# Two graph layers on one core: the order of VectorE's work within a turn, and of the last steps

## Chip, cores, metric

The kernel runs on one core of a Trainium2 chip. The metric is device time in microseconds (us), the median of three runs of the whole program. A core has five engines that run their own instruction streams and wait for one another by semaphores: TensorE (PE in the profile; its weight loads are PEld), VectorE (DVE), ScalarE (ACT), GpSimd (POOL) and SyncE (SP, which here only issues transfers).

## The reference

64 graphs of 256 nodes with 256 features go through two layers. Everything is 32-bit floating point.

```
layer 0, per graph:  h = x
  twice:  Wh = h @ W;  e = leaky_relu(Wh @ a[:F] + (Wh @ a[F:]).T)
          h = softmax(where(adj > 0, e, -9e15), axis=1) @ Wh
  h = layernorm(x + h);  h = layernorm(h + relu(h @ w_ff1 + b_ff1) @ w_ff2 + b_ff2)
layer 1, per graph:  8 heads of 32 features
  attn = softmax(q k^T / sqrt(32));  out = sum_r (attn * (adj == r)) @ (src @ Wv[r])
  x = layernorm(src + out @ Wo);     layernorm(x + gelu(x @ W1 + b1) @ W2 + b2)
```

The adjacency holds zeros and ones only, so of the four relations of layer 1 two occur. The kernel uses that, and tests on the chip whether it holds; with other data a general path would run.

## The kernel before

**Tiling.** Two graphs make a pair: 512 nodes, which is T = 4 blocks of 128 partitions (NB = 2 blocks per graph, G = 2 graphs). There are NG = 32 pairs.

**Pipeline over turns.** `turn(y_, x_, z)` runs three pairs at once: layer 1 of pair `y_`, the feed-forward part of layer 0 of pair `x_ = y_ + 1`, and the two attention steps of layer 0 of pair `z = y_ + 2`. In the code capital `Y`, `X`, `Z` are the dictionaries of these pairs; near the end `X` or `Z` is None. `middle` is true in turns 1 to 30, in which `X` exists and `y_` isn't 0. Ahead of turn 0 stands a prologue that loads weights and brings pairs 0 and 1 to the point where turn 0 expects them; it spreads the folding of norm weights into the next weights over its waits (`next(fold)`). An output norm that a turn leaves open is put on `waiting` and finished in the next turn.

**Products with seven multiplications.** Large products are computed block-wise with seven products in place of eight. `hidden_seven` makes the hidden layer of a feed-forward part: it subtracts quarters of the features first (`sub`, line 881, tile `tt`), and then goes through named steps. A digit names a product and a letter the half of the hidden features: "2a" is product 2 for half a. Two banks of PSUM per half, `one` and `two` (tiles `h1a` and `h1b`), take the products; after each product the bank is copied by ACT (line 911) or added by DVE (line 908, `taken`), and the next product of the same bank is accumulated on top of what is there, so it can't start before that copy or addition has read the bank. Products 1, 6, 7, 4 share bank `one`, products 2, 5, 3 bank `two`. "ra", "sa", "ca", "da" are activations on ACT. `Projections` does the same for q, k ("q1" and so on) and v ("v1" and so on), with DVE additions at line 1039 and ACT copies at line 1042. `HiddenOut` makes the second half of a feed-forward part; its `sums` are DVE operations at line 974, its `add` is line 996.

**Attention of layer 1.** There are four quads (graph b, half m of the heads), numbered 0 to 3. `scores(n)` is the score product (`sp`, line 1075) and the exponential on ACT (`e`, line 1084); `masks(n, (a,))` multiplies two heads by the adjacency on DVE (`ea`, line 1088, one instruction of 128x1024); `totals(n)` adds the two node blocks (`es`, line 1093); `sums(n)` are the products with v (`po`, line 1103, first with `e`, then with `ea`) and, last, with ones (`zo`, line 1106, from `es`); `shares(b)` divides.

**Norms.** `moments` runs bn_stats and bn_aggr on DVE (lines 826, 827), per block of 128 rows; `norm` calls it for the blocks not yet done and then computes the reciprocal root on GpSimd (lines 837, 838, and 840 for the last norm); `offsets` is one small DVE instruction (`nm`, line 845) that needs the root; `applied_norm` applies mean and root per block on ACT (line 855) or, on request, on GpSimd (line 852). `affine` multiplies by the norm's weight and adds its bias on DVE (lines 864, 867, 128x1024 each).

**Transposed features.** `normed_features` transposes 32x32 blocks on DVE (line 694), and twelve SyncE transfers and four GpSimd copies put the blocks in place (tile `hT`). `to_features` does it with TensorE transposes (line 674) and two copies out of PSUM (line 675), one by ACT and one by DVE unless told otherwise. `with_ones` then sets one row of 512 to one, a memset on GpSimd (line 686): that row carries the bias.

**What sets the order.** `tc.manual_schedule` fixes the order of the code on the engines that it lists. In turns 0 to 30 these are PE, SP, DVE and ACT; in turn 31 and in the prologue PE and SP. Engines that aren't listed are ordered by a planner with its own costs; GpSimd always is.

In a middle turn the code gives the following order in the part that edits 1 to 3 of the change touch (shortened; a bar separates steps, dots stand for left-out ones):

```
            scores(0, (0, 1)) ... v5 q6, v6, masks(0, (0,))
            q3 q7 | masks(0, (2,)) | v7 | totals(0) | v3 q4 v4
            first_hidden (four subtractions) | norm(w, 3, wy) | scores(1)
            masks(1, (0,)) | offsets | masks(1, (2,)) | totals(1) | sums(0) | 2a 1a .. 5a ..
            scores(2) | sums(1) | 6a | shares(0) | 3a | masks(2, (0,)) | 2b ra 1b 7a
            masks(2, (2,)) | 5b sa 6b 4a | totals(2) | 3b rb 7b
```

Of the kernel before, what the change touches and what calls it, by code (L numbers as in the profile page):

```python
# [385 lines left out]
def narrow_path(  # L386
# [281 lines left out]
    def to_features(src, name, copies=(nc.scalar.copy, nc.vector.tensor_copy)):  # L668

        dst = work.tile([P, KB, TN], F32, tag="hT", name=name)  # L670
        for k in range(KB):
            ps = bank(f"{name}p{k}")
            for t in range(T):
                nc.tensor.transpose(ps[:, t * P:(t + 1) * P], src[:, t, k * P:(k + 1) * P], ident)
            copies[k](dst[:, k, :], ps)  # L675
        return [dst[:, k] for k in range(KB)]
# [7 lines left out]
    def with_ones(hT):  # L684

        nc.gpsimd.memset(hT[KB - 1][one], 1.0)
        return hT
# [142 lines left out]
    def norm(u, l, y, blocks=range(T), mv=None, rest=range(NB, T)):  # L830

        n, t0 = f"{u}_{l}_{blocks[0]}", blocks[0]
        bt = slice(t0, t0 + len(blocks))
        mv = moments(u, l, y, blocks if mv is None else rest, mv)
        rs = work.tile([P, T], F32, tag="rs", name=f"rs{n}")
        nm = work.tile([P, T], F32, tag="nm", name=f"nm{n}")
        nc.gpsimd.tensor_scalar(rs[:, bt], mv[:, bt, 1], EPS, 0.0, op0=ALU.add, op1=ALU.add)  # L837
        nc.gpsimd.tensor_tensor(rs[:, bt], rs[:, bt], mhalf[:, bt], ALU.pow)  # L838
        if l == 3:
            nc.gpsimd.tensor_add(high[:, bt], high[:, bt], mv[:, bt, 0])  # L840
        return blocks, mv, rs, nm
# [5 lines left out]
    def applied_norm(y, blocks, mv, rs, nm, part=None, gpsimd=False):  # L847
        if part is None:
            offsets(blocks, mv, rs, nm)
        for t in part or blocks:  # L850
            if gpsimd:
                nc.gpsimd.tensor_scalar(y[:, t, :], y[:, t, :], rs[:, t:t + 1], nm[:, t:t + 1],
                                        op0=ALU.mult, op1=ALU.add)
                continue
            mark["normed"] = nc.scalar.activation(y[:, t, :], y[:, t, :], AF.Identity,  # L855
                                                  bias=nm[:, t:t + 1], scale=rs[:, t:t + 1])

    def affine(y, g_, b_):

        times(y, g_)  # L860
        plus(y, b_)
# [145 lines left out]
    class Projections:  # L1007
# [17 lines left out]
        def out(s, x, o, b):  # L1025
            if x == "q":
                return s.qk[:, o, :, b * N:(b + 1) * N]
            return s.v[:, b * NB:(b + 1) * NB, o * F:(o + 1) * F]
# [173 lines left out]
    def first_hidden(x_):  # L1202

        X = g[x_]
        hT = X["hT"]
        if x_ == 0:
            hT = [h.rearrange("p (t a r) -> p t a r", t=T, r=32) for h in hT]
        X["h1"] = work.tile([P, FB, TN], F32, tag="h1", name=f"h1{x_}_0", bufs=1)
        tt = work.tile([P, Q, KB, T, 32], F32, tag="yt", name=f"tt{x_}_0", bufs=1)
        return hidden_seven(x_, 0, hT, wf1s, bf1, AF.Relu, X,  # L1210
                            tt.rearrange("p q k t r -> p (q k t r)"))
# [5 lines left out]
    def turn(y_, x_, z):  # L1217
# [9 lines left out]
        def scores(n, heads=range(HPB)):  # L1227
            pe[n], e[n] = weighted(y_, *quads[n], q, k_, Y["aT"])
            powers(n, heads)
# [4 lines left out]
        def masks(n, *pairs):  # L1234
            masked(*e[n], *pairs)
# [10 lines left out]
        def shares(b):  # L1246
            divided(y_, b, *acc[b], oT)
# [5 lines left out]
        def first(names, ends=0):  # L1253

            if X:
                steps(names)
            else:
                for _ in range(ends):
                    piece()
# [3 lines left out]
                                            ("PE", "SP", "DVE", "Activation")[:4 if X else 2]})  # L1263
        with order:
            p.sums()
            if X:
                n = X.pop("n")
                offsets(*n)
# [35 lines left out]
            if X:  # L1304
                masks(0, (0,))
            if middle:
                p("q3 q7")
                masks(0, (2,))
                p("v7")
            else:  # L1310
                p("q6 v6 q7 v7")
                if X:
                    masks(0, (2,))
# [4 lines left out]
                    masks(0)  # L1318
                    totals(0)
            p("v3 q4 v4" if middle else "q4 v4")  # L1320
            steps = first_hidden(x_) if X else None
            if waiting:
                last = norm(w, 3, wy, mv=last)
            scores(1)
            masks(1, (0,))
            if waiting:
# [19 lines left out]
            if not X:  # L1346
                with behind("out"):
                    shares(0)
            masks(2, (0,))
            first("2b ra 1b 7a")  # L1350
            masks(2, (2,))
            first("5b sa 6b 4a")
            totals(2)
# [44 lines left out]
            if Z:  # L1398
                out(1)
                Z["m"].scores(0)  # L1400
                Z["m"].scores(1)
                Z["m"].exp(0)
                Z["m"].exp(1)
                out.sums(4)
                offsets(*n)
                out(2)
                applied_norm(y, *n, range(T))
                Z["m"].masks(0)
                out(5)
                Z["m"].masks(1)  # L1410
                Z["m"].shares()
            elif X:
                out(5)
                out.sums(3)
            if not Z:
                applied_norm(y, *n)
            else:
                Z["m"].scaled(WH)
                nc.scalar.activation(work.tile([P, 1], F32, tag="ve", name=f"ve{y_}"), mhalf[:, 0:1], AF.Gelu)
# [36 lines left out]
            if Z:  # L1456
                second("2a 1a")
                n = norm(x_, 1, X["y"], mv=n, rest=range(NB + 1, T))
                second("2b 1b ca 6a")
                offsets(*n)  # L1460
                applied_norm(X["y"], *n, [0])
                applied_norm(X["y"], *n, [2, 3], True)
                second("5a")
                applied_norm(X["y"], *n, [1])
                affine(y, rg3, rb3)
                second("6b 5b cb")
                X["hT"] = normed_features(x_, 1, X["y"], natural=True)
                second("7a 7b sa sb 3a da 3b db 4a 4b")
            else:
                if X:  # L1470
                    n = norm(x_, 1, X["y"], mv=n, rest=range(NB + 1, T))
                second("2a 1a 2b 1b")
                second("5a 5b")
                if X:
                    applied_norm(X["y"], *n)
                second("3a 3b 6a 6b ca cb da db 7a 7b")
                if X:
                    affine(y, rg3, rb3)
                    X["hT"] = with_ones(to_features(X["y"], f"h2T{x_}", (nc.vector.tensor_copy,) * 2))
                second("sa sb 4a 4b")  # L1480
            if y_ >= NG - 2:
                pieces = out_pieces(y_, y, h1)
                if X:
                    left.append(pieces)
                    affine(X["y"], rg2, rb2)
                else:
                    for _ in pieces:
                        pass
                return
# [25 lines left out]
            out(4)  # L1515
            waiting.append((y_, y))

    waiting = []

    with tc.manual_schedule(engines={mybir.EngineType.PE, mybir.EngineType.SP}):  # L1520
        for stage in (early_first, project, first_softmax):
            stage(0)
        early_first(1)
        next(fold)
        for stage in (project, first_softmax):
            stage(1)
        first_sums(0)
        next(fold)
        second_softmax(0)
        first_sums(1)  # L1530
        next(fold)
        second_softmax(1)
        for b in range(G):
            second_sums(0, (b,))
            normed(0, 0, g[0]["y"], range(b * NB, (b + 1) * NB))
        next(fold)
        g[0]["hT"] = to_features(g[0]["y"], "h1T0")
        for u in range(2):
            checked(u, g[u]["aq"])
        affine(g[0]["y"], rg1, rb1)  # L1540
        load_x(2)
        load_rows(2)
        load_adjacency(2)
        first_hidden(0)("2a 1a 2b 1b 5a 5b 3a 3b 6a ra 6b rb 7a sa 7b sb 4a 4b")
        first = HiddenOut(0, 0, g[0]["y"], g[0]["h1"], wf2s, out_sums(0, 0))
        first.sums(1, 2, 4, 3)
        first(1, 2, 5, 6, 3)
        normed(0, 1, g[0]["y"], range(NB))
        first(7, 4)
        normed(0, 1, g[0]["y"], range(NB, T))  # L1550
        g[1]["n"] = norm(1, 0, g[1]["y"], mv=second_sums(1))
        g[0]["hT"] = with_ones(to_features(g[0]["y"], "h2T0"))
        affine(g[0]["y"], rg2, rb2)
        next(fold)
        for u in range(NG):
            turn(u, u + 1, u + 2)
# [54 lines left out]
```

## Time and profile before

| | |
|---|---|
| median of 3 runs | 3021.93 us (3021.1 to 3023.58) |
| the profiled execution's own time | 3021.42 us |
| its span in the profile | 3019.7 us |
| granted TensorE clock | 0.995 |
| PE busy | 2965.3 us (98%), 22192 instructions |
| DVE busy | 2609.3 us (86%), 5025 instructions |
| ACT busy | 1729.2 us (57%) |
| POOL busy | 642.9 us (21%) |
| prologue, start of turn 0 (first product at line 1055) | 103.5 us |
| turn 0 | 98.2 us |
| turns 1 to 29 | 90.9 to 92.9 us each, mean 91.6 |
| turn 30; turn 31 to the end | 75.9 us; 86.8 us |

A turn is taken in the timeline from its first matmul at line 1055 to that of the next turn. In a timeline each line holds the start in us, the time from the first start to the last end of equal instructions in a row, the engine, the line of the kernel, the operation, the tiles written and read with their shapes, the count, and in brackets how long the engine was idle just before and who ended that. Matmuls overlap: an entry of four matmuls of 128x256 is 1.03 us long when they start 0.216 us apart and the last takes 0.379 us, and the next entry then begins 0.86 us after it. A matmul that starts later than that has waited, even where the entries still overlap and no idle time is printed.

### The profile page before, as it was taken

Reading aid. Unit: us, or ns where it says so; the run is one execution under the profiler, and the core shown is the slowest. Engines: PE = TensorE matmul, PEld = TensorE weight load, DVE = VectorE, ACT = ScalarE, POOL = GpSimd, SP = SyncE. Lnnn points to the kernel's source line nnn. Section 1 sums busy time; section 2 is a strip of 40 time slices with the busy share of each in tenths; the row PEclk is TensorE's granted clock in tenths of the full one; section 3 lists DMA queues with packets and bytes.
Section 4 is the critical chain, followed back from the end, with each engine's and each line's share of the span. In section 5 each row is a group of like instructions: output and inputs, shape, how many; then the busy total and the mean of one; then the engine's idle time right before and its main releaser. Section 6 shows DMA issues by size and latency. Waiting matters only on the chain.

```text
span 3019.7 us, 58579 instructions
## 1 busy us (share of the span) xinstructions
PE 2965.3 (98%) x22192; PEld 2492.9 (83%) x22192; DVE 2609.3 (86%) x5025; ACT 1729.2 (57%) x3564; POOL 642.9 (21%) x928
## 2 busy tenths in 40 slices
PE   7999999999999999999999999999999999999998
PEld 6788888888888888888888888888888888888876
DVE  5788888889888889898889888898988898888887
ACT  4455655655655656565555556556556555555553
POOL 4222211222211222211222112222112222112211
PEclk8999999999999999999999999999999999999999
DMA  5011111211111211112111112111112111121000
GB/s 149 13 31 41 38 39 25 45 38 40 36 30 36 45 37 40 33 27 43 38 41 37 39 26 45 38 40 37 34 33 45 38 40 33 27 43 38 22 10 16
DMA packets 428404, 113.26 MB, mean 38 GB/s; under 512 B 364586, under 2 KB 427604, under 8 KB 428116
## 3 DMA queue, kind: packets, MB, share of 16 engines
q1 hardware_dynamic: 418076, 102.20, 15.5%
q10 hardware_dynamic: 8984, 6.19, 0.8%
q8 instruction: 178, 2.92, 0.4%
q0 software_dynamic: 1056, 1.05, 0.1%
q14 instruction: 110, 0.90, 0.1%
HBM read 56.78 MB, written 16.78 MB: 24 GB/s over the span
## 4 chain that ended last, share of the span: by engine, by line
PE 76%; DVE 13%; SPq 4%; issue 2%; DMA 2%; POOL 2%; ACT 1%; ACTq 0%; DVEq 0%; POOLq 0%
PE yf L988 25%; PE h1a L899 12%; PE h1b L899 8%; PE po L1103 5%; SPq L713 4%; PE v L1055 4%; PE qk L1055 4%; PE xpp L740 4%; PE yop L811 4%; PE hpp L800 3%; PE ygp L811 3%; PE sp L1075 2%; DVE ea L1088 2%; DVE h L908 2%; PE zo L1106 1%
## 5 line engine op out<-in xcount | busy, mean ns | idle before, releaser
L855 ACT ACTIVATE y<-y,nm,rs 128x256 f32<-128x256 f32 x452 | 243.5, 592 | 142.3 <-DVE nm L845 137.9
L1088 DVE TENSOR_TENSOR ea<-e,aT 128x1024 f32<-128x1024 f32 x256 | 307.3, 1212 | 2.8 <-ACT e L1084 2.8
L1084 ACT ACTIVATE e<-sp 128x512 f32<-128x512 f32 x512 | 270.5, 596 | 27.4 <-PE sp L1075 20.8
L911 ACT COPY h<-h1b 128x512 f32<-128x512 f32 x262 | 152.3, 582 | 199.1 <-PE h1b L899 196.7
L837 POOL TENSOR_SCALAR rs<-mv 128x4 f32<-128x4 f32 (+1 forms) x134 | 56.6, 422 | 968.3 <-DVE mv L827 787.6
L917 ACT ACTIVATE h<-h,cols 128x256 f32<-128x256 f32 x512 | 221.7, 501 | 38.9 <-DVE h L908 38.1
L1042 ACT COPY qk<-qk 128x512 f32<-128x512 f32 x128 | 74.4, 581 | 291.9 <-PE qk L1055 291.9
L711 POOL COPY hT<-yt 32x256 f32<-32x256 f32 x244 | 211.4, 867 | 140.2 <-DVE yt L694 129.0
L826 DVE BATCH_NORM_STATS2 st<-y 128x6 f32<-128x256 f32 x512 | 208.1, 408 | 5.6
L908 DVE TENSOR_TENSOR h<-h1a,h 128x512 f32<-128x512 f32 x262 | 173.1, 679 | 40.8 <-PE h1a L899 33.0
L996 DVE TENSOR_TENSOR y<-yf,y 128x256 f32<-128x256 f32 x448 | 184.7, 412 | 17.1 <-PE yf L988 16.6
L1116 POOL TENSOR_TENSOR low<-low,rq 128x16 f32<-128x16 f32 x64 | 14.0, 218 | 740.1 <-DVE rq L1115 740.1
L867 DVE TENSOR_TENSOR y<-y,rb 128x1024 f32<-128x1024 f32 (+1 forms) x130 | 167.0, 1284 | 3.2
L742 ACT COPY xp<-xpp 128x260 f32<-128x260 f32 x128 | 45.5, 386 | 195.1 <-PE xpp L740 195.0
L864 DVE TENSOR_TENSOR y<-y,rg 128x1024 f32<-128x1024 f32 (+1 forms) x130 | 155.8, 1198 | 1.2 <-ACT y L855 1.1
L1093 DVE TENSOR_TENSOR es<-e 128x1024 f32<-128x1024 f32 x128 | 155.7, 1216 | 0.0
L838 POOL TENSOR_TENSOR rs<-rs,mhalf 128x4 f32<-128x4 f32 (+1 forms) x134 | 146.8, 1095 | 8.3
L1075 PE MATMUL sp<-qk 32*128 32x256 f32 x2048 | 146.6, 400 | 0.0
L1103 PE MATMUL po<-ea,v 128*32 128x256 f32 x2048 | 137.8, 379 | 0.8 <-DVE ea L1088 0.7
L1103 PE MATMUL po<-e,v 128*32 128x256 f32 x2048 | 136.3, 384 | 0.0
L899 PE MATMUL h1a<-tt,wf 128*128 128x256 f32 x512 | 131.3, 380 | 0.0
L740 PE MATMUL xpp<-gwe,xT 128*128 128x260 f32 x512 | 128.4, 395 | 2.0 <-ACT xT L675 2.0
(284 smaller groups left out, 7648.9 us busy)
## 6 DMA issues: line engine op xcount, KB each, us to landing
hT<-yt SPq DMA_DIRECT2D x912, 32.0 KB, 1.9
y<-in_x_dram SPq DMA_DIRECT2D x32, 512.0 KB, 4.7
xq<-in_x_dram SPq DMA_DIRECT2D x240, 64.0 KB, 2.2
aq<-in_adj_dram SPq DMA_DIRECT2D x240, 64.0 KB, 2.4
out_dram<-y SPq DMA_DIRECT2D x30, 512.0 KB
hT<-yt ACTq DMA_DIRECT2D x180, 32.0 KB, 1.9
wf<-in_L_gnn_w_ff_dram SPq DMA_DIRECT2D x2, 1024.0 KB, 7.4
w<-in_L_gnn_W_dram SPq DMA_DIRECT2D x2, 1024.0 KB, 7.7
```

The source lines that it names most:

```text
L711: nc.gpsimd.tensor_copy(to, at)
L740: nc.tensor.matmul(ps[:, :WX], hT[k][:, t * P:(t + 1) * P], gwe[:, k, :], start=(k == 0), stop=(k == KB - 1))
L811: nc.tensor.matmul(ps[:, i * F:(i + 1) * F], lhs(t, k), rhs(b, k), start=(k == 0), stop=(k == n - 1))
L855: mark["normed"] = nc.scalar.activation(y[:, t, :], y[:, t, :], AF.Identity, bias=nm[:, t:t + 1], scale=rs[:, t:t + 1])
L899: nc.tensor.matmul(ps[:, i * N:(i + 1) * N], w_[:, f * P:(f + 1) * P], m, start=first and i == 0, stop=True, skip_group_check=True)
L908: mark["added"] = nc.vector.tensor_tensor(out(h, o, b), pair(ps), out(h, o, b), ALU.add)
L917: nc.scalar.activation(y, y if ps is None else ps[:, i * N:(i + 1) * N], func, bias=bi[:, f:f + 1])
L988: nc.tensor.matmul(s.ps[n][:, i * F2:(i + 1) * F2], a[:, k, i * P:(i + 1) * P], w_[:, k, :], start=n in (1, 2, 5) and i == 0 and k == 0, s ...
L1055: nc.tensor.matmul(ps[:, i * N:(i + 1) * N], l, r, start=n in (1, 2, 5) and i == 0, stop=True, skip_group_check=True)
L1084: nc.scalar.activation(e[:, a, :], ps[a], AF.Exp, scale=isd)
L1088: nc.vector.tensor_tensor(ea[:, a:a + 2, :], e[:, a:a + 2, :], ab[:, None, :].to_broadcast([P, 2, NB * N]), ALU.mult)
L1103: nc.tensor.matmul(po[hp, m * N:(m + 1) * N], vs[:, hp], w[:, a, j * N:(j + 1) * N], start=(n == 0), stop=(n == len(terms) - 1))
```

## The change

Seven edits.

1. In the middle turns the second half of quad 0's masks goes behind the addition of v7 on DVE.
2. In the middle turns the last norm's remaining statistics (`norm(w, 3, ...)`: two bn_stats and two bn_aggr on DVE, three small operations on GpSimd) go ahead of the four feature subtractions of `first_hidden`.
3. In turns 0 to 30 the first half of quad 2's masks goes behind the addition of 1b and ahead of that of 7a.
4. In turn 30 `sums(3)` of the feed-forward output goes between product 5 and its addition.
5. In turn 30 the norm of pair 31 isn't applied by four ACT operations in a row: block 0 and block 1 stay on ACT, ahead of the copies of 3a and 3b, and blocks 2 and 3 go to GpSimd.
6. The affine steps of the prologue (pair 0) and of turn 30 (two of them) are kept on a list, `late`, and are written behind the feature subtractions of the next turn's `Projections`. In turn 31, where DVE isn't ordered by hand, the planner places them: in the built program one of turn 30's two affine steps then stands in the middle of turn 30, around the first bn_stats of pair 31, and the other among turn 31's feature subtractions.
7. In the prologue both copies of `to_features` are on ACT; in the built program the memset of the ones row then stands on GpSimd between the two scalings of `w1` (line 603) and no longer behind both.

```diff
             p.sums()
+            while late:
+                affine(*late.pop(0))
             if X:
                 n = X.pop("n")
                 offsets(*n)
...
             if middle:
-                p("q3 q7")
+                p("q3 q7 v7")
                 masks(0, (2,))
-                p("v7")
...
             p("v3 q4 v4" if middle else "q4 v4")
-            steps = first_hidden(x_) if X else None
             if waiting:
                 last = norm(w, 3, wy, mv=last)
+            steps = first_hidden(x_) if X else None
             scores(1)
...
+            first("2b ra 1b")
             masks(2, (0,))
-            first("2b ra 1b 7a")
+            first("7a")
             masks(2, (2,))
...
             elif X:
-                out(5)
+                out.product(5)
                 out.sums(3)
+                out.add(5)
...
                 second("5a 5b")
                 if X:
-                    applied_norm(X["y"], *n)
-                second("3a 3b 6a 6b ca cb da db 7a 7b")
+                    offsets(*n)
+                    applied_norm(X["y"], *n, [0])
+                second("3a")
                 if X:
-                    affine(y, rg3, rb3)
+                    applied_norm(X["y"], *n, [1])
+                second("3b")
+                if X:
+                    applied_norm(X["y"], *n, [2, 3], True)
+                second("6a 6b ca cb da db 7a 7b")
+                if X:
                     X["hT"] = with_ones(to_features(X["y"], f"h2T{x_}", (nc.vector.tensor_copy,) * 2))
...
                 if X:
                     left.append(pieces)
-                    affine(X["y"], rg2, rb2)
+                    late.append((y, rg3, rb3))
+                    late.append((X["y"], rg2, rb2))
...
-    waiting = []
+    waiting, late = [], []
...
-        g[0]["hT"] = with_ones(to_features(g[0]["y"], "h2T0"))
-        affine(g[0]["y"], rg2, rb2)
+        g[0]["hT"] = with_ones(to_features(g[0]["y"], "h2T0", (nc.scalar.copy,) * 2))
+        late.append((g[0]["y"], rg2, rb2))
```

The order of TensorE's matmuls and of SyncE's transfers is the same in both programs.

## Prediction

> **What bounds the kernel now.** The page comes first, for who is busy:
>
> ```profile
> PE 2965.3 (98%) x22192; PEld 2492.9 (83%) x22192; DVE 2609.3 (86%) x5025; ACT 1729.2 (57%) x3564; POOL 642.9 (21%) x928
> ```
>
> PE is the bound, and idle for 54 us, but busy entries overlap. So I read matmul starts in the timeline: four products of 128x256 take 0.86 us, and a later next entry has waited. Laying turns 1 to 29 over each other, the shortest (turn 9) has 90.92 us and the mean is 91.57. Three places in turn 16 show where PE waits for DVE. First, v4, in PE's timeline and then DVE's:
>
> ```profile
> 1587.32 1.03 PE L1055 MATMUL qk<-tq,wqk 128*128 128x256 f32 x4
> 1588.27 1.13 PE L1055 MATMUL v<-wv,tq 128*128 128x256 f32 x4
> ```
> ```profile
> 1585.00 1.48 DVE L1039 TENSOR_TENSOR qk<-qk,qk 128x512 f32<-128x512 f32 x2 [1.40 <-PE qk L1055]
> 1586.40 1.22 DVE L1088 TENSOR_TENSOR ea<-e,aT 128x1024 f32<-128x1024 f32 x1
> 1587.53 0.68 DVE L1039 TENSOR_TENSOR v<-v,v 128x512 f32<-128x512 f32 x1
> ```
>
> v4 is due at 1587.32 + 0.86 = 1588.18. It starts at 1588.27, 0.06 after the addition of v7 has left its bank at 1588.21. Its entry lasts 1.13 in place of 1.03: after a wait the second matmul starts 0.32 after the first, not 0.216. So this costs 0.09 + 0.10 = 0.19, in all of turns 1 to 30. The addition stood behind a mask.
>
> Second, the stretch around the transposed features, on DVE and then PE:
>
> ```profile
> 1591.17 0.43 DVE L881 TENSOR_TENSOR tt<-hT 128x256 f32<-128x256 f32 x1 [1.22 <-issue]
> ...
> 1592.64 0.42 DVE L826 BATCH_NORM_STATS2 st<-y 128x6 f32<-128x256 f32 x1
> ...
> 1593.72 1.19 DVE L1088 TENSOR_TENSOR ea<-e,aT 128x1024 f32<-128x1024 f32 x1
> 1596.19 0.16 DVE L845 SCALAR_TENSOR_TENSOR nm<-mv,rs 128x4 f32<-128x4 f32 x1 [1.27 <-POOL rs L838]
> 1596.27 1.22 DVE L1088 TENSOR_TENSOR ea<-e,aT 128x1024 f32<-128x1024 f32 x1
> 1597.41 1.22 DVE L1093 TENSOR_TENSOR es<-e 128x1024 f32<-128x1024 f32 x1
> ```
> ```profile
> 1597.53 1.07 PE L1103 MATMUL po<-ea,v 128*32 128x256 f32 x16
> 1598.68 0.64 PE L1106 MATMUL zo<-es,ones 128*32 128x256 f32 x8
> ```
>
> DVE waits for the transfers of `hT` (in the list of waits, tt waits 55 us for DMA over the kernel), then works through everything behind it, waiting 1.27 more for GpSimd's root. `zo`, due at 1598.39, waits for `es`. The transfers land between 14.76 us (turn 9) and 16.11 us (turn 4) after the turn's start, 16.82 in turn 30; turn 4 is 1.36 us longer than turn 9. From here to 6b DVE leads and PE follows.
>
> Third, 6b, on PE and then DVE:
>
> ```profile
> 1603.70 1.03 PE L899 MATMUL h1b<-tt,wf1s 128*128 128x256 f32 x4
> 1605.12 1.13 PE L899 MATMUL h1a<-tt,wf1s 128*128 128x256 f32 x4 [0.39 <-DVE h L908]
> ```
> ```profile
> 1603.25 1.21 DVE L1088 TENSOR_TENSOR ea<-e,aT 128x1024 f32<-128x1024 f32 x1
> 1604.38 1.28 DVE L908 TENSOR_TENSOR h<-h1a,h 128x512 f32<-128x512 f32 x2
> ```
>
> 6b is due at 1604.56 and starts 0.56 late, as the addition of 1b stood behind a mask. Even turn 9 loses 0.16 here, and 0.10 at the second matmul.
>
> **The Trainium skill.** "Perfetto Trace Analysis", section Identifying the Most-Contended Engine, says that matmul busy share doesn't measure the distance to the limit; the trace agrees (98% busy, yet the waits above). "TensorE: Matmul & The Clock Gate", section Step-by-step, has matmuls in program order with only weight loads pulled ahead: one late addition holds everything behind. In the trace nothing overtakes v4 or 6b. "SBUF — State Buffer", section Who interferes with whom, has DVE and GpSimd sharing a port pair as an exclusive lock. The trace fits: GpSimd's first root operation (line 837) took 1.00 us beside a mask at 1594.00, but 0.24 at 1576.95; in the prologue DVE's `nm` took 1.23 beside a GpSimd addition, not 0.16.
>
> **Edit 1, v7 ahead of the mask.** v7's product begins at 1585.59. An addition follows its product's begin by 1.07 (7b in turn 0: 140.36 and 141.43), so at 1586.66, done at 1587.34: v4 doesn't wait. Gain 0.19 x 30 turns = 5.8 us. DVE now idles some 0.2 for v7; mask, `es` and v3's addition come 0.26 later, the latter at 1589.52. The mask is needed by `po` at 1591.29 only.
>
> **Edit 2, statistics first.** They take 1593.72 - 1592.64 = 1.08 us. Behind v3's addition they run from 1590.2 to 1591.3, in the wait for `hT`. The subtractions start when both are there, 1591.3 (before 1591.17); 5a needs the first of them at 1594.53. The mask of quad 1 starts 1.47 after them, 1592.7 in place of 1593.72. GpSimd's three operations are moved past nothing of its own, since its queue is empty; they took 2.4 from the last statistic to `nm`, so the root is there at 1593.8, when the mask ends. Then `es` runs 1595.1 to 1596.3, 2.3 earlier, and `zo` (due 1598.2) waits no more. If the port keeps GpSimd out until the mask is done, `nm` waits its 1.27 again and `es` ends at 1597.6, still in time. Even with transfers as late as 16.1, `zo` is met. What goes is the excess over turn 9 between `hT` and 6b: on average 0.19 at `zo` and 0.26 at 6b, 0.44 x 29 = 12.9, plus 1.6 in turn 30: 14.5 us.
>
> **Edit 3, 1b ahead of the mask.** With DVE no longer late, 1b's addition begins 1.07 after its product and ends at +1.75; 6b is due at +2.59 and doesn't wait. Gain beside that of edit 2: 0.26 x 30 = 7.8 us. Behind the waiting addition stands the mask, and behind that 7a's addition, which 4a waits for: 1.07 + 0.60 + 1.13 + 0.68 = +3.48, and 0.06 to the start, +3.54. 4a is due at 4 x 0.864 = +3.46. **This is a new wait**: 0.08 + 0.10 = 0.18 in turns 0 to 30, a loss of 5.7 us. It could be nothing (-0) or, if 1b's addition is late by some tenths, twice that.
>
> **Edits 4 to 7.** Edit 4 costs nothing: `nm` at 2909.50 waits for GpSimd's root, and the next addition is behind it. Edit 7 and the prologue's part of 6: at 108.98 PE has waited 1.80 for the ones row, which stood behind 4.47 us of weight scaling. It now stands behind half of that, near 106.6. Then q5 waits for q2's addition, behind two affine instructions on DVE (2.4 us) and `nm`. Nothing to 1.8; I take 0.5, as `nm` comes hardly earlier. The second copy costs ACT 0.59, inside its idle 3.38. Edits 5 and 6 in turn 30: 7a waited 1.89 at 2927.15 for copies behind four ACT norms (2.07), and q1 waited 1.26 at 2933.01 for copies behind an affine. Both shrink, but the affine now in turn 30's middle puts 2.3 us of DVE ahead of the subtractions: 5a, due at 2919.84, waits some 1.5, and GpSimd's two blocks (1.48 each in earlier turns) end near 2928.8, ahead of the transposes. Between 2 lost and 1 gained; I take 0.
>
> **Sum.** 5.8 + 14.5 + 7.8 - 5.7 + 0.5 = 22.9, of the profiled execution's own 3021.42 (span 3019.7): 2998.5. The median is 0.5 above that execution: 2999 us.
>
> **Rivals.** (a) *The gain is partly given back at 4a* (chance 0.15). Where 1b's addition starts late, because the division ahead of it does, the mask between makes 4a wait as long as 6b did. For it: every instruction from 1591 to 1606 on DVE hangs together. Against: the 2 us of reserve at `es`. Then 7.8 and about a third of 14.5 are lost: 3012. (b) *No change, the transfers are next* (0.08). In 5 of 29 turns the first product of the second hidden layer waits 0.3 to 1.4 us for `hT`, on average 0.12. If PE arrives 0.75 earlier and the features don't, it waits there: 3021. Against: `tt` and the norm behind it move with PE, as both follow 7b. (c) *Slower, by the same transfers* (0.06). They share SyncE's queue with the next pair's loads; if the new times make them meet in every turn, each waits like turn 8 (1.36). It decides from a mean wait of 0.12 + 0.75 + 0.2 = 1.1 us per turn; at 1.36 the cost is 1.24 x 29 = 36, less 22.9: 3035. Nothing in the trace makes it likely. (d) The change doesn't do what it says: the affine step was to move behind turn 31's subtractions and lands in turn 30. That is in the sum; with GpSimd holding the port it costs 4, 3003. It belongs to the main case.
>
> **Numbers.** A measurement tells about 0.2%, 6 us, from no change. Main case 0.71: 2993 (no wait at 4a) to 3006 (twice that wait, and turn 30's 2 us). With (a) the range is 2992 to 3014. Faster 0.86, same 0.08, slower 0.06.
>
> **What would show it.** In the profile after: v4 0.86 behind q4; no wait of `zo`; 6b 0.86 behind 5b; 4a some 0.95 behind 6b, with an entry of 1.13; all middle turns within 0.1 of 90.65 except for the waits on `hT`. Turns still spread by the transfers' times would refute edit 2's account, a 4a later than 1.2 behind 6b that of edit 3.

## The result, and the profile after

| | before | after |
|---|---|---|
| median of 4 runs | 3022.76 us (3021.1 to 3026.34) | 3003.71 us (3001.51 to 3007.76) |
| ratio of after to before | | 0.9937, 95% interval 0.992 to 0.9954 |
| the profiled execution: own time; span | 3021.42; 3019.7 us | 3007.76; 3006.1 us |
| start of turn 0 | 103.5 us | 103.7 us |
| turn 0 | 98.16 us | 100.45 us |
| turns 1 to 29: shortest; mean; sum | 90.92; 91.57; 2655.5 us | 90.73; 91.07; 2641.1 us |
| turn 30; turn 31 to the end | 75.86; 86.7 us | 74.08; 86.8 us |

The change gains 19 us by the medians; 22.9 were predicted. The profiled execution after is the slowest of its four runs, 4.05 us above their median, which has to be kept in mind when its sums are read. It gains only 13.6 us of span, 14.4 of them in turns 1 to 29 and 1.8 in turn 30, while turn 0 loses 2.3 and the prologue 0.2.

In the page of the kernel after, first busy time and then the chain of waits that ended last:

```profile
PE 2952.3 (98%) x22192; PEld 2493.3 (83%) x22192; DVE 2614.8 (87%) x5024; ACT 1728.7 (58%) x3563; POOL 622.7 (21%) x930
...
PE 90%; DVE 5%; DMA 2%; ACT 1%; issue 1%; POOL 1%; SPq 0%; ACTq 0%; POOLq 0%; DVEq 0%
```

PE's share of the busy time is again 98%, so the busy line shows nothing of the gain. The chain does: before, it gave PE 76% and DVE 13%, since it was so often followed back through a late addition or mask.

Turn 16 again, in the timeline of PE:

```profile
1582.15 1.03 PE L1055 MATMUL qk<-tq,wqk 128*128 128x256 f32 x4
1583.01 1.03 PE L1055 MATMUL v<-wv,tq 128*128 128x256 f32 x4
...
1592.17 1.05 PE L1103 MATMUL po<-ea,v 128*32 128x256 f32 x16
1593.04 0.61 PE L1106 MATMUL zo<-es,ones 128*32 128x256 f32 x8
...
1598.00 1.03 PE L899 MATMUL h1b<-tt,wf1s 128*128 128x256 f32 x4
1598.86 1.03 PE L899 MATMUL h1a<-tt,wf1s 128*128 128x256 f32 x4
1599.89 1.13 PE L899 MATMUL h1a<-tt,wf 128*128 128x256 f32 x4
```

v4 stands 0.86 behind q4, `zo` 0.87 behind `po`, 6b 0.86 behind 5b: the three waits of before are gone. 4a, the last line, comes 1.03 behind 6b instead of 0.86, and its entry is 1.13 long: the new wait, 0.17 + 0.10 = 0.27 us. And in the timeline of DVE:

```profile
1581.56 0.69 DVE L1039 TENSOR_TENSOR v<-v,v 128x512 f32<-128x512 f32 x1 [0.24 <-PE v L1055]
1582.16 1.22 DVE L1088 TENSOR_TENSOR ea<-e,aT 128x1024 f32<-128x1024 f32 x1
...
1586.41 0.44 DVE L881 TENSOR_TENSOR tt<-hT 128x256 f32<-128x256 f32 x1 [0.22 <-issue]
...
1589.06 0.15 DVE L845 SCALAR_TENSOR_TENSOR nm<-mv,rs 128x4 f32<-128x4 f32 x1
...
1590.27 1.21 DVE L1093 TENSOR_TENSOR es<-e 128x1024 f32<-128x1024 f32 x1
...
1593.72 0.72 DVE L1114 STREAM_TRANSPOSE rz<-zo 128x512 f32<-128x512 f32 x1 [0.48 <-PE zo L1106]
...
1597.41 0.69 DVE L908 TENSOR_TENSOR h<-h1a,h 128x512 f32<-128x512 f32 x1 [0.62 <-PE h1a L899]
1598.02 1.22 DVE L1088 TENSOR_TENSOR ea<-e,aT 128x1024 f32<-128x1024 f32 x1
1599.15 0.68 DVE L908 TENSOR_TENSOR h<-h1a,h 128x512 f32<-128x512 f32 x1
```

`nm` waits for no root any more, and `es` is done 1.5 us ahead of `zo`. DVE now waits for PE at `rz` (a transpose of what `zo` made) and at 1b's addition, where before PE waited for DVE. The last three lines are the new wait: 1b's addition, the mask and 7a's addition run without a gap, the last ends at 1599.83, and 4a starts 0.06 later.

Of turns 1 to 29, 21 now take 90.73 or 90.74 us; the scatter with the arrival of the first `hT` of a turn is gone. What is left in the other eight is mostly waits of one later product, the first of layer 1's second feed-forward part, for the transfers of its `hT`. In PE's timeline of turn 1:

```profile
268.92 1.10 PE L899 MATMUL h1b<-hT,w 128*128 128x256 f32 x4 [2.38 <-DMA hT<-yt]
```

and 0.23 us per turn on average, after 0.11 before. (Turns 21 and 25 lose 0.3 to 0.4 us later, at line 988; such losses stood in eight turns before, too.) Turn 0 is taken up with the experiments, since its loss was not foreseen.

### The profile page after: what moved, and what is told of

The parts are those of the page before. It is cut to its first block, busy times and chain, and to the rows that moved or that the text cites. A ratio compares the mean times of both kernels' runs of the same rounds, so it can differ in the third digit from the quotient of the medians.

```text
span 3006.1 us, 58577 instructions
## 1 busy us (share of the span) xinstructions
PE 2952.3 (98%) x22192; PEld 2493.3 (83%) x22192; DVE 2614.8 (87%) x5024; ACT 1728.7 (58%) x3563; POOL 622.7 (21%) x930
## 4 chain that ended last, share of the span: by engine, by line
PE 90%; DVE 5%; DMA 2%; ACT 1%; issue 1%; POOL 1%; SPq 0%; ACTq 0%; POOLq 0%; DVEq 0%
PE yf L988 24%; PE h1a L899 15%; PE h1b L899 11%; PE po L1103 7%; PE v L1055 7%; PE qk L1055 6%; PE sp L1075 4%; PE ygp L811 3%; PE xpp L740 3%; PE yop L811 3%; PE hpp L800 3%; PE zo L1106 2%; PE rows L749 1%; DMA hT<-yt 1%; DVE st L826 0%
## 5 line engine op out<-in xcount | busy, mean ns | idle before, releaser
L837 POOL TENSOR_SCALAR rs<-mv 128x4 f32<-128x4 f32 (+1 forms) x134 | 34.2, 255 | 908.7 <-DVE mv L827 544.5
L1075 PEld LDWEIGHTS sp<-qk 32*128 32x128 f32 x2048 | 93.0, 185 | 45.3 <-issue 22.2
```

Of the source, the lines that this page charges most:

```text
L1075: nc.tensor.matmul(ps[a][:, j * N:(j + 1) * N], k_[hp, m, j0:j0 + P], q[hp, m, b * N:(b + 1) * N], start=True, stop=True)
```

## The experiments

Each ratio is that to the kernel before, timed beside the run. The median of before was 3021.9, 3024.4 or 3024.1 us there, so between groups of runs ratios are to be compared, not medians. They resolve some 0.1% (3 us) of the whole time; what is smaller is read from the lengths of turns. In the middle turns without a wait on `hT` these repeat to 0.01 us once DVE has ceased to set them.

**One edit of the three at a time.** The traces suggested that the three edits of the middle turns don't add as in the prediction's sum. The reading: from `hT` to 6b DVE leads, so that a microsecond saved on PE ahead of that stretch (edit 1) is waited away at `zo` or 6b, and only edit 2 takes DVE out of the lead; edit 3 then has nothing left to gain at 6b and only brings 4a's wait. The rival is the prediction's sum itself.

Edit 1 alone:

```diff
-                p("q3 q7")
+                p("q3 q7 v7")
                 masks(0, (2,))
-                p("v7")
```

> Edit 1 alone, the rest as before. Theory A (the shares of the prediction add up): v4 follows q4 by 0.86, each of turns 1 to 30 is 0.19 us shorter, 5.8 us in all. Theory B (from the transfers of hT to product 6b DVE leads, and its times hang on the transfers alone): v4 is early in the same way, but 6b starts where it did, since the addition of 1b comes no earlier; turns 1 to 29 keep their mean of 91.6 us, and the time stays within 1.5 us of the kernel before.

Measured: ratio 0.9992 (0.9983 to 1.0), 3020.4 us; turns of 90.92 to 92.45 us. PE's timeline in turn 16 of this kernel, q4 and v4, then 5b and 6b:

```profile
1586.96 1.03 PE L1055 MATMUL qk<-tq,wqk 128*128 128x256 f32 x4
1587.82 1.03 PE L1055 MATMUL v<-wv,tq 128*128 128x256 f32 x4
...
1603.32 1.03 PE L899 MATMUL h1b<-tt,wf1s 128*128 128x256 f32 x4
1604.74 1.13 PE L899 MATMUL h1a<-tt,wf1s 128*128 128x256 f32 x4 [0.39 <-DVE h L908]
```

v4 is on time, and 6b is late all the same. Even the shortest turn has kept its 90.92: there 6b comes 1.22 behind 5b, before 1.02, so the wait moved from v4 to 6b. Over turns 1 to 29 nearly all of the 0.19 us saved at v4 come back: 0.08 more on average at `zo` and the masked products ahead of it, and 0.09 more at 6b. The ratio leaves 0 to 5 us of gain; the 5.8 us of the prediction are not there.

Edit 2 alone:

```diff
-            steps = first_hidden(x_) if X else None
             if waiting:
                 last = norm(w, 3, wy, mv=last)
+            steps = first_hidden(x_) if X else None
```

> Edit 2 alone. Theory A: the waits of zo go and the scatter of the turns goes, but 6b still waits 0.16 behind the mask: 14.5 us shorter. Theory B: once DVE isn't late, the addition of 1b ends about 28.0 us after the turn's start even behind the mask, ahead of 6b's due time of 28.5, so 6b doesn't wait either; the turns without a wait on the second hT have 90.92 - 0.26 = 90.66 us, and the kernel is some 21 us shorter (2.5 either way for the waits on the second hT, which differ from run to run).

Measured: ratio 0.9927 (0.9913 to 0.994), 2999.3 us. In turn 16 of its profile, q4 and v4, then 5b, 6b and 4a:

```profile
1576.68 1.03 PE L1055 MATMUL qk<-tq,wqk 128*128 128x256 f32 x4
1577.64 1.13 PE L1055 MATMUL v<-wv,tq 128*128 128x256 f32 x4
...
1592.73 1.03 PE L899 MATMUL h1b<-tt,wf1s 128*128 128x256 f32 x4
1593.59 1.03 PE L899 MATMUL h1a<-tt,wf1s 128*128 128x256 f32 x4
1594.46 1.03 PE L899 MATMUL h1a<-tt,wf 128*128 128x256 f32 x4
```

v4 still waits (0.96 behind q4, entry 1.13). 6b is on time although the mask still stands ahead of 1b's addition, and 4a is on time too. 22 of the turns 1 to 29 have 90.65 or 90.66 us, less than the shortest turn before. This one edit is worth all of the change's gain: 0.9927 and the change's 0.9937 can't be told apart by the times, and its turns are 0.07 us shorter than the changed kernel's.

DVE's `rz` in turn 16 shows who leads. The kernel before, then edit 2 alone:

```profile
1600.30 0.67 DVE L1114 STREAM_TRANSPOSE rz<-zo 128x512 f32<-128x512 f32 x1
```
```profile
1588.45 0.72 DVE L1114 STREAM_TRANSPOSE rz<-zo 128x512 f32<-128x512 f32 x1 [1.01 <-PE zo L1106]
```

Before, DVE has no idle time there; with edit 2 it waits 1.01 us for PE. The edit has two parts: 1.08 us of statistics leave the stretch behind `hT`, and `nm` no longer waits 1.27 us for the root. In turn 16 `nm` comes 18.21 us after the turn's start instead of 20.51, about the sum of both. Whether one part alone would have been enough was not tried.

Edit 3 alone:

```diff
+            first("2b ra 1b")
             masks(2, (0,))
-            first("2b ra 1b 7a")
+            first("7a")
```

> Edit 3 alone. The statistics still stand behind the subtractions, so DVE's times from there on hang on the transfers of hT and the turns still scatter with them. 6b doesn't wait, but 4a waits for the addition of 7a, whose place in DVE's order is the same as before. Theory A: 0.26 less at 6b and 0.18 to 0.27 more at 4a, so within 3 us of the kernel before. Theory B: before, 4a followed 6b by 0.97 and was itself 0.4 later than the addition of 7a allowed; now it starts with that addition, so 0.1 to 0.3 per turn are gained, 3 to 8 us; the long waits of zo stay.

Measured: ratio 0.9987 (0.998 to 0.9993), 3017.44 us; turns of 90.92 to 92.2 us. 6b is freed, but PE still waits at `zo` or at the masked products just ahead of it in 7 turns, by up to 1.2 us, and 4a, which comes at least 1.02 behind 6b, comes 1.07 to 1.38 behind it in 16. By the times it gains 3.9 us (2.1 to 6.0), where the sum had 7.8 less the 5.7 of the new wait. So alone, edit 3 is a gain.

The change without edit 3:

> The changed kernel without edit 3 (mask of quad 2 ahead of 1b again). Theory A (edit 3 takes the wait of 6b away): 6b waits 0.26 again and 4a no longer 0.27, no difference from the changed kernel. Theory B (edit 2 alone frees 6b, edit 3 adds only the wait of 4a): neither 6b nor 4a waits, the middle turns without a wait on hT fall from 90.73 to 90.46, and the kernel is some 8 us shorter than the changed one, about 2995.

Measured: ratio 0.991 (0.9894 to 0.9925), 2994.44 us; 22 of the turns 1 to 29 have 90.46 to 90.48. In turn 16, 5b, 6b and 4a:

```profile
1591.50 1.03 PE L899 MATMUL h1b<-tt,wf1s 128*128 128x256 f32 x4
1592.36 1.03 PE L899 MATMUL h1a<-tt,wf1s 128*128 128x256 f32 x4
1593.22 1.03 PE L899 MATMUL h1a<-tt,wf 128*128 128x256 f32 x4
```

All three follow at 0.86. Against the changed kernel's 90.73 that is 0.27 us in each turn, 4a's wait exactly. With edit 2 in place, edit 1 does bring its 0.19 (90.66 to 90.47), and edit 3 costs 0.27 x 31 = 8 us; the ratios, 0.991 and 0.9937, differ by as much.

**Turn 0 and the ends.** Turn 0 after the change, PE's timeline and then DVE's:

```profile
105.84 1.13 PE L1055 MATMUL qk<-h2T,wqk 128*128 128x256 f32 x4 [0.18 <-POOL h2T L686]
...
111.90 2.07 PE L1055 MATMUL qk<-tq,wqks 128*128 128x256 f32 x4 [4.07 <-DVE qk L1039]
113.90 2.09 PE L1075 MATMUL sp<-qk 32*128 32x256 f32 x16
115.92 1.72 PE L1055 MATMUL v<-wvs,tq 128*128 128x256 f32 x4
117.47 1.03 PE L1055 MATMUL qk<-h2T,wqks 128*128 128x256 f32 x4
```
```profile
106.83 1.21 DVE L864 TENSOR_TENSOR y<-y,rg 128x1024 f32<-128x1024 f32 x1
108.08 2.02 DVE L867 TENSOR_TENSOR y<-y,rb 128x1024 f32<-128x1024 f32 x1
110.03 1.22 DVE L845 SCALAR_TENSOR_TENSOR nm<-mv,rs 128x4 f32<-128x4 f32 x1
111.17 0.68 DVE L1039 TENSOR_TENSOR qk<-qk,qk 128x512 f32<-128x512 f32 x1
```

q2 comes at 105.84 instead of 108.98: the wait for the ones row has shrunk from 1.80 to 0.18. But q5 waits 4.07 us for q2's addition, behind the two instructions of the affine step and a `nm` of 1.22 us. Then three entries last nearly twice as long as elsewhere. The windows show why: behind the bounds and the length each line has the busy times (and counts) of PE, PEld, DVE, ACT and POOL, and then the clock granted to PE. After, from 108 on:

```profile
108.00:111.00 3.00, 0.00 (x0) 0.00 (x0) 2.97 (x3) 0.00 (x0) 2.92 (x2) 0.89 0.00 0
111.00:118.00 7.00, 6.10 (x27) 4.19 (x28) 3.01 (x7) 3.59 (x7) 5.52 (x8) 0.56 0.03 7
```

The clock is halved for the work that follows the wait. In the trace's clock records the half-clock stretch goes from 110.32 to 117.14, 6.83 us, two of 3.41; in all profiles the half-clock stretches of the prologue and turn 0 are multiples of 3.41. The Trainium skill ("TensorE: Matmul & The Clock Gate", section What's actually happening) states that after an idle window of about 3.4 us the clock falls to a half, until PE has been busy for such a window; this fits in part. In turn 0 of the thirteen profiles each of the eight waits of 3.34 to 4.07 us has a half-clock stretch that begins within 1.7 us of the wait's end, and no wait up to 2.83 us has one. But here the clock fell 2.49 us after the wait's begin (107.83), sooner than a whole window. And the kernel before has a stretch as well (103.59 to 107.01), with no such wait ahead of it; it falls on q1 and v1:

```profile
103.52 1.99 PE L1055 MATMUL qk<-h2T,wqk 128*128 128x256 f32 x4
105.31 1.87 PE L1055 MATMUL v<-wv,h2T 128*128 128x256 f32 x4
```

There it cost little, since PE waited for the ones row afterwards anyway. In the four kernels with one of edits 1 to 3 alone or with turn 30's part alone, whose prologue is that of before, q1 and v1 are at full clock, PE waits 3.49 to 3.56 us for the ones row, and the stretch comes behind that wait.

Edits 4 to 7 alone (edits 1 to 3 left out):

> This kernel is the one before with edits 4 to 7 alone (the ones row, the affine steps of the first and last turns); edits 1 to 3 are left out. Theory A (the prediction's sum for these edits): 0.5 us gained, 3021.4 us, turn 0 shorter by about 0.5. Theory B (from the traces so far: turn 0 of the changed kernel is 2.3 us longer because q5 waits about 4 us for VectorE, which stands behind the two late affine instructions, and the products after the wait run at half clock; turn 30 is 0.8 us shorter by these edits): turns 1 to 29 as before, 90.9 to 92.9 us, turn 0 about 100.3 us with q5's wait near 4 us, net 3021.9 + 2.0 - 0.8, some 3023 us (3021 to 3025).

Measured: ratio 0.999 (0.9983 to 0.9996), 3021.16 us beside 3024.37 for before. Its turn 0 is 99.38, q5 waits 4.07 us, turn 30 is 75.28, its span 3021.6. The trace agrees with Theory B in its waits, but turn 0 has only one half-clock stretch of 3.41 us and is 0.9 shorter than said; the time, 3 us below that of before beside it, agrees with neither theory, though the bare number lies in Theory B's range. The next runs split the edits.

The changed kernel with the prologue as before:

```diff
-        g[0]["hT"] = with_ones(to_features(g[0]["y"], "h2T0", (nc.scalar.copy,) * 2))
-        late.append((g[0]["y"], rg2, rb2))
+        g[0]["hT"] = with_ones(to_features(g[0]["y"], "h2T0"))
+        affine(g[0]["y"], rg2, rb2)
```

> This kernel is the changed one with the affine of the prologue put back (edit 7 and the prologue's part of edit 6 undone), all else kept. Theory A (turn 0's loss comes from something else, such as the orders of edits 1 to 3): turn 0 stays at 100.4 us and the time at 3003 us. Theory B (it is the affine on VectorE ahead of q5's doubling): turn 0 goes back to 98.2 to 98.8 us, turns 1 to 29 stay at 90.73, the time is about 2 us below the changed kernel, 3001.5 us (2999.5 to 3003).

Measured: turn 0 98.47 us, middle turns 90.73, span 3002.2 (3.9 below the changed kernel's); ratio 0.993 (0.9916 to 0.9944), which doesn't tell it from the changed kernel. In the trace q5's wait is back at 1.22, as in Theory B; a gain of 2 us is below what the timing resolves.

The prologue's part alone, on the kernel before:

> This kernel is the one before with edit 7 and the prologue's part of edit 6 alone; turn 30 is left as before. The profile of edits 4 to 7 together had turn 0 at 99.4 us (before 98.2) and turn 30 at 75.3 (before 75.9), but its runs were 0.1% faster than before, which the profile doesn't show; this run and its sister with turn 30's part tell which of the two the profile has wrong. Theory A (the prologue's part gains, and the profile caught an unlucky turn 0): turn 0 at or below 98.2 us, the time 1 to 3 us below before. Theory B (the affine's two instructions and the long normalisation ahead of q5's doubling cost more than the earlier ones row brings): q5 waits about 4 us, turn 0 is 99.4 to 100.4 us long depending on how much of the half-clock window falls behind the wait, the time 1 to 2 us above before or not to be told from it; and the 0.1% was chance.

Measured: ratio 1.0 (0.9992 to 1.0008); turn 0 starts late, at 104.6, and takes 97.69 us, with a wait of q5 of 2.83. Here the entries behind the wait are at full clock:

```profile
112.84 1.13 PE L1055 MATMUL qk<-tq,wqks 128*128 128x256 f32 x4 [2.83 <-DVE qk L1039]
113.90 1.15 PE L1075 MATMUL sp<-qk 32*128 32x256 f32 x16
```

The half-clock stretch had fallen on q1 and v1 (104.7 to 108.1) and so shortened the wait. So the length of turn 0 alone misleads; the end of turn 0 counts. It lies at 201.2 to 202.7 us in the six kernels with the prologue of before (middle 201.8), and at 202.3 to 204.4 in the four with the changed one (202.3, 203.0, 204.1, 204.4; middle 203.6). By these middles the prologue's part costs about 1.7 us, while single profiles differ by nothing to 3, and the timing of this run allows from a loss of 2.4 to a gain of 2.4.

Turn 30's part alone, on the kernel before:

> This kernel is the one before with edits 4 and 5 and turn 30's part of edit 6; the prologue is left as before. Theory A (the 0.1% of edits 4 to 7 comes from here): turn 30 is 3 us shorter than before, 72.9 us. Theory B (the traces so far): turn 30 is 0.6 to 0.8 us shorter than before, 75.0 to 75.3, with a wait of 5a near 1.4 us and no wait of q1 in turn 31; turn 0 is 98.2 to 98.7; the time is 0.5 to 1 us below before, which can't be told from no change.

Measured: ratio 0.9993 (0.9985 to 1.0001); turn 30 74.91 us, 5a waits 1.42, q1 of turn 31 no more. These are the waits of Theory B: 1.89 at 7a and 1.26 at q1 before, 1.42 at 5a and 0.77 at 7a now, 0.96 less. The length of turn 30 says less, since it follows the transfers: with the prologue's part alone turn 30 is unchanged, its `hT` landed 15.30 us after its start instead of 16.82, and it took 74.35. The two parts together don't explain the 3 us of edits 4 to 7 by any wait that the profiles show; chance is likely at this resolution, but not shown.

**Towards a faster version.** On top of the change without edit 3, turn 0's affine is moved behind `nm` and the additions of q2 and v2:

```diff
             p.sums()
-            while late:
+            while late and y_:
                 affine(*late.pop(0))
...
                 X["hT"] = normed_features(x_, 0, X["y"])
+            while late:
+                affine(*late.pop(0))
```

> This kernel is the changed one without edit 3, and turn 0's late affine stands on VectorE behind the normalisation and the additions of q2 and v2 instead of ahead of them; so q5's doubling comes at about 107.9 us instead of 111.9. To be read against the changed kernel without edit 3 (2994.4 us, turn 0 of 100.2). Theory clock (the slow q5, sp and v5 of turn 0 are TensorE at half clock after the 4 us of idle time): without that idle time there is no half-clock window, the entries of q5, sp and v5 fall from 2.07, 2.09 and 1.72 us to about 1.13 each, turn 0 takes 94 to 95 us, the time is about 2989 us. Theory side work (they are slow because GpSimd and the copies run beside them): the entries stay near 2 us, only the 4 us of wait go, turn 0 takes 96 to 97 us, about 2990.5 us.

Measured: ratio 0.9891 (0.9876 to 0.9906), 2992.8 us, turn 0 96.65. PE's timeline: q1 and v1, then q5, then q7.

```profile
104.13 2.04 PE L1055 MATMUL qk<-h2T,wqk 128*128 128x256 f32 x4
105.96 1.83 PE L1055 MATMUL v<-wv,h2T 128*128 128x256 f32 x4
...
109.51 1.13 PE L1055 MATMUL qk<-tq,wqks 128*128 128x256 f32 x4
...
118.04 1.13 PE L1055 MATMUL qk<-tq,wqk 128*128 128x256 f32 x4 [1.73 <-DVE qk L1039]
```

q5 doesn't wait and runs at full clock beside the same GpSimd work (POOL busy for 2.84 of the 3 us from 108), so the side work is not what slowed it: the entries are those of the clock theory. But that theory had no half-clock stretch without the wait, and there is one: it falls on q1 and v1 (104.2 to 107.6). And the moved affine, again long (2.18 at line 867), holds up an addition that q7 needs for 1.73 us. So the turn's length is that of the other theory after all. The trace gains 3.6 us in turn 0 (100.21 to 96.65).

Turn 30's affine in the hand order, behind the last additions of turn 30, on top of that:

```diff
                     left.append(pieces)
-                    late.append((y, rg3, rb3))
+                    affine(y, rg3, rb3)
```

> This kernel is the one with turn 0's affine moved, and turn 30's affine written in the hand order behind the last additions of turn 30 instead of ahead of the subtractions of its last sums. To be read against that kernel. Theory A (the wait of 1.43 us of the 5a block in turn 30 for tt is the affine's two instructions ahead of the subtractions): the wait goes, turn 30 is about 1.4 us shorter, and nothing comes back in turn 31; about 2987.5 us. Theory B (VectorE has no room in that stretch: the affine stands ahead of what the first query block of turn 31 needs instead): 5a's wait goes but turn 31's first products wait 1 to 1.5 us longer; no difference that can be measured.

Measured: ratio 0.9884 (0.9869 to 0.9899), 2990.39 us; turn 30 71.64 instead of 73.77. The 5a and 7a blocks, with the change and then with this kernel:

```profile
2908.52 1.97 PE L899 MATMUL h1b<-tt,w1s 128*128 128x256 f32 x8 [1.43 <-DVE tt L881]
...
2914.78 2.10 PE L899 MATMUL h1a<-tt,w 128*128 128x256 f32 x8 [0.77 <-DVE h L908]
```
```profile
2892.36 1.89 PE L899 MATMUL h1b<-tt,w1s 128*128 128x256 f32 x8
...
2898.20 2.10 PE L899 MATMUL h1a<-tt,w 128*128 128x256 f32 x8 [0.41 <-DVE h L908]
```

5a's wait is gone, 7a's is smaller, and turn 31 to the end takes 86.8 us as in the kernel that it is read against: Theory A. By its median this is the fastest kernel here, 1.2% below before, where the change is 0.6% below; from the kernel with turn 0's affine moved (0.9891) only the trace tells it apart.

The same kernel with the affine of pair 0 back in the prologue, the copies still on ACT:

> This kernel is the fastest so far (edits 1 and 2, turn 0's affine behind the normalisation, turn 30's affine in the hand order) with the affine of pair 0 back in the prologue, but both copies of to_features still on ACT. There the planner puts the two affine steps ahead of the prologue's last feature subtractions. To be read against that kernel, whose turn 0 is 96.7 us long and has a wait of 1.72 us of the first product after q4 and v4 for VectorE, behind the affine. Theory A (VectorE has room ahead of the subtractions, since it waits 0.7 us for the ones row anyway): the wait of 1.7 us goes and q2 comes at most 1 us later, turn 0 is about 95.5 us, the time about 1 us below, 2989.5. Theory B (the affine runs at double length beside GpSimd, as it did in turn 0, and delays the subtractions by 2 to 3 us): q2 waits 2 us, turn 0 is 96.7 us or more.

Measured: ratio 0.9899 (0.9883 to 0.9914), 2993.29 us, turn 0 99.87. Neither theory as it was put: q2 doesn't wait, but `nm` comes at 111.02 (0.93 of waiting for GpSimd's root, 1.22 long), q5 waits 3.34 us behind it, and a half-clock stretch follows from 114.5 on. The affine did run long, as Theory B said (2.00 at line 867). In the trace q5's wait, and with it the loss, comes from `nm`'s lateness; by the times (0.9899 and 0.9884) the two kernels can't be told apart.

## Why the prediction was right, and where it was wrong

**The sign, the size and the range** held: 2999 predicted, 3003.7 measured, inside 2992 to 3014. What carried it is the reading of the three places in turn 16: all three waits went, and most middle turns took 90.73 where 90.65 was said. That parts of the sum were booked to the wrong edits, as follows, hardly touched the total: 6b's 0.26 us stand in it once, whichever edit frees it. It mattered for the advice, since it made edit 3 look like a gain beside edit 2.

**Edit 2's account held, its size was too small.** `nm` at the mask's end, `es` early, `zo` on time: as worked out. But 14.5 us were booked to it, and 6b's remaining 0.26 to edit 3. Edit 2 alone frees 6b in every turn, since 1b's addition was late not only by the mask ahead of it but because all of DVE's work since `hT` was: in the kernel before DVE shows no gap from `es` to 6b, with edit 2 it waits for PE at `rz`. So the excess over turn 9 was the wrong measure: turn 9 itself was held up. On the average of turns 1 to 29, 0.19 us at `zo` and 0.52 at 6b went, 20.5 us in all, and turn 30 is 1.7 us shorter. (In turn 30 6b was never late; there the sum counted one turn too many.)

**Edit 1's 5.8 us** show only with edit 2: alone no gain that can be told from none, on top of edit 2 0.19 us per turn. The sum took waits of one engine one behind the other as independent; while DVE leads further down, an earlier PE only waits longer there.

**Edit 3 was the step that failed most.** Its 7.8 us were already gained by edit 2, and its new wait was sized at 0.18 us where 0.27 was measured: 1b's addition begins 1.14 after its product (1596.27 and 1597.41 in turn 16), not 1.07 as taken from one place in turn 0; why, no run shows. Everything behind it comes as worked out, 0.07 to 0.08 later. The step foresaw the wait, its place and the term of 0.10 for the second matmul; the balance of the edit was +2.1 in the sum and is about -8 measured beside edit 2 (0.27 x 31), though +3.9 alone.

**Edits 4 to 7.** The step said nothing to 1.8 us gained in turn 0, and took 0.5. In its own words "q5 waits for q2's addition, behind two affine instructions on DVE (2.4 us) and `nm`". That chain is right, but its durations were taken from undisturbed rows: the second affine step took 2.02 instead of 1.22 and `nm` 1.22 instead of 0.16, both beside GpSimd's work on the weights (lines 603 and 573). The Trainium skill ("SBUF — State Buffer", section Who interferes with whom), which the prediction had cited for just such a `nm`, warns of it: a DVE instruction with two inputs from SBUF contends with a GpSimd instruction that reads SBUF. The trace before had the prices, 1.94 us for this affine instruction in its prologue and 1.23 for `nm`. And the half clock was not in the sum at all. Turn 30's net of 0 was close: its printed waits are 0.96 less with edits 4 to 6, and with edits 1 and 2 beside them it takes 73.74 where edit 2 alone has 74.20, of which edit 1 is 0.19; its length varies by more than that with the transfers.

**The account.** The profile's gain of 13.6 is 9.3 short of the 22.9: 0.09 x 29 = 2.6 at 4a; 2.8 in the prologue and turn 0 (2.5 lost, where the sum, with its 0.18 at 4a, had 0.3 gained); 3.5 for the waits on `hT` of the second feed-forward part, (0.23 - 0.11) x 29; 0.2 in turn 30 and behind it. These make 9.1; the rest is rounding. The medians lack only 3.9, since that of before lies 1.3 above its profiled execution and that of after 4.05 below. The waits on `hT` are rival (b) in a small measure. In the other profiles that term varies from 0.05 to 0.17 per turn; its mean is 0.09 in the six profiles without edit 2 and 0.14 in the seven with it, 1.4 us in all. So most of the 3.5 us is probably not the change's; the unprofiled runs can't show it.

**The rivals.** (a) named the right place, 4a, but not the reason: the wait is a constant 0.27, not a late division. (c) didn't occur. (d) was right in the trace: one affine step of turn 30 lands in the middle of turn 30 and costs 5a its 1.43, as the kernel with that affine in the hand order shows by removing it. That 3003.7 us is close to this rival's 3003 is chance: the losses lie at 4a and in turn 0.

## What to carry to other kernels

Where two in-order engines wait for each other in turns, find the stretch in which one of them has no gap of its own: only work removed or moved there counts as long as that is so, and a wait removed ahead of it comes back at its end. Test edits one by one, and beside each other: here one reordering of four statistics was worth the whole change, and another, which gains 4 us alone, costs 8 beside it. A fixed new wait is sized to some hundredths of a microsecond only from the same place of the same turn, and in a loop of 31 turns 0.1 us is 3 us.

## What the runs showed of the hardware

A wait of PE of about 4 us was paid for twice: the entries of the products behind it took 2.07, 2.09 and 1.72 us in place of 1.13, 1.15 and 1.13. The half-clock stretches are multiples of 3.41 us. In turn 0 each of the eight waits of 3.34 us or more has such a stretch within 1.7 us of its end: after 3.34 and 3.49 to 3.56 us one of 3.41, after 4.07 one of 3.41 (edits 4 to 7 alone) or 6.83 (the whole change, with and without edit 3). After 2.83 us there was none. But a wait of 1.89 us, that of 7a in turn 30, was followed by one in two of the five profiles that have it (edit 1 alone and edit 3 alone, 1.1 to 1.2 us behind the wait's end), and these two have the longest turn 30, 76.52 and 77.19 us. So where the stretches fall isn't set by the wait alone, and what else sets it stays open.

GpSimd's first root operation (line 837) took 0.23 us with DVE's masks out of its way and 1.00 beside one; over the kernel the mean of its 128x4 form fell from 424 to 234 ns. Edit 2 brings the two apart: the root is now computed beside the feature subtractions.
